# A graph attention layer over sorted edges: the dense part for the first 128 groups is taken out, and feature tiles come free by whole batches

## The chip, the cores and the metric

The kernel runs on one core of a Trainium2 chip. Its time is the device time of one execution in microseconds; the time before is the median of three runs, 6012.39 us (6009.27 to 6016.66). The profile is of one execution, with a line for each instruction: PE is the matrix engine (PEld its weight loads), DVE the vector engine, ACT the scalar engine, POOL the engine that issues the indirect DMAs (gathers), SP an engine that here only issues DMAs.

## The reference

There are 12500 nodes with 64 features, 400000 edges with 64 features each, and the edges are sorted by their destination. The density of destinations falls along the nodes: the first groups of 512 edges lie on a few nodes, the last on some 30.

```python
h_src = nfeats[src]
h_dst = nfeats[dst]
z_att = concatenate([h_src, h_dst, efeats])
e = leaky_relu(z_att @ W_attn + b_attn, 0.01)
m = concatenate([h_src, efeats]) @ W_ne
alpha = exp(e - segment_max(e, dst)[dst]) / segment_sum(exp(...), dst)[dst]
z = segment_sum(alpha * m, dst)
out = layernorm(nfeats + relu(concatenate([nfeats, z]) @ W_out))
```

## The kernel before

The edges are cut into 782 groups of 512 (128 partitions by T = 4; the last group has 128 edges). `sorted_path` (line 48) does the whole work where the destinations are sorted and no group spans more than S = 48 nodes; it leaves a flag, and a second function, `general_path`, runs after it only if the flag is set.

*Setup.* The node table is read, the parts of the score that belong to a node (as source, as destination) are computed, and a table of 65 columns (features and source score) is written to DRAM. A second table in DRAM, `shifted`, holds for each node the destination scores of the 48 nodes from it on; seven gathers (line 525) take from it the window of each group's first node, `wins`.

*Sparse groups.* Groups 127 to 781 (655 of them) go through the loop at line 756 in batches: 16, then 31 of 20 (`BS`), 11 and 8. A batch is worked in parts of `SG` = 4 groups. For each part:

- `gather` (line 199) loads the edges' features `ze` by SP and issues 16 indirect DMAs on POOL, 4 per group, which fetch the table rows of the sources into `zx` (line 214). `ze` and `zx` come from the pool `feats` with `ZB` = 8 buffers each. In the built program each gather also waits for the gather eight before it.
- `scores` (line 220) multiplies `ze` by the edge weights and sums (232, 234), adds the source score (239), marks each edge's destination in a one-hot tile `hot` (241), multiplies it with the window `win` (246) that ACT has copied, and sums (249).

When all parts of a batch have scores, `softmax` (line 294) works on the whole batch: scans along the edges give the maximum and the sum of each destination, and carry over from batch to batch; the weights `alpha` are left in PSUM. Then `aggregate` (line 401) runs part by part: `w` = `hot` times `alpha` on DVE (404, two buffers), 32 products on PE with `ze` and `zx` as weights (412) into `pg` (four PSUM buffers, which other work uses too), and for each group one addition of 48 columns into the accumulator `acc` on DVE (422).

`prepare` (line 739) makes a batch's index lists, two batches ahead: a load, a conversion on ACT, a subtraction on DVE, eight transposes on PE.

*Dense groups.* The first 128 groups never gather: `dense_part` (line 586) is a generator that takes the sources' scores and features from the node table by one-hot products on PE (lines 633, 675, 697), with its own softmax and its own accumulator `acc_d`, merged into `acc` at its end. The loop over the sparse batches takes a step of it after each part's scores, at times two, and one after each part's sums.

*Finishing.* `finish` (line 543) takes four blocks of 128 nodes (25 such blocks of work): transposes of x, products with the output weights, normalisation, and the store. It is due when no later edge can touch its nodes; `due` is computed from the expected distribution of the destinations, and a limit on the actual one is checked into the flag.

The order of the instructions on each engine is laid out by a scheduler when the program is built; each engine then works through its own queue in order.

Of the kernel before, what the change touches and what calls it, by code (L numbers as in the profile page):

```python
# [15 lines left out]
P = 128  # L16
T = 4
# [14 lines left out]
ZB = 8  # L32
HB = 7

DENSE = ((32, 2, (32,)), (32, 2, (13, 10, 9)), (32, 3, (7, 7, 6, 6, 6)), (32, 3, (5, 5, 5, 5, 4, 4, 4)))
KD = 128
ND = 8
NT = 3
NA = 30
NDW = 392  # L40
# [7 lines left out]
def sorted_path(ctx, tc, x, dst, idx, edge, w_ne, w_attn, b_attn, w_out, out, flag):  # L48

# [15 lines left out]
    assert REST == P and NG % BG and sum(G for G, _, _ in DENSE) == KD <= P  # L69
# [18 lines left out]
    slots0 = const.tile([P, P], F32, name="slots0")  # L88
    nc.gpsimd.iota(slots0, pattern=[[1, P]], base=0, channel_multiplier=0,
                   allow_small_or_imprecise_dtypes=True)  # L90
    lane = const.tile([P, 1], F32, name="lane")
    nc.gpsimd.iota(lane, pattern=[[0, 1]], base=0, channel_multiplier=1,
                   allow_small_or_imprecise_dtypes=True)
    ident16 = const.tile([BG, BG], BF16, name="ident16")
    nc.vector.tensor_copy(ident16, ident[0:BG, 0:BG])
    ss = const.tile([P, NB], F32, name="ss")
    ofs = const.tile([1, KD * T], I32, name="ofs")
    at0 = const.tile([1, KD], I32, name="at0")
    acc_d = const.tile([P, NDW], F32, name="acc_d")

# [8 lines left out]
    d0i = const.tile([1, NG], I32, name="d0i")  # L109
    worst = const.tile([P, 2], F32, name="worst")  # L110
    odd = const.tile([1, 4], F32, name="odd")
# [9 lines left out]
    fixed2 = psum.tile([P, 512], F32, name="fixed2", bufs=1)  # L121
# [6 lines left out]
    casts = []  # L128

    def indices(g0, G, dense=False):  # L130

# [11 lines left out]
        lows = None  # L143
        if dense:
            low = dn.tile([P, T, P], F32, name="lot", bufs=2).bitcast(I32)
            nc.vector.tensor_scalar(low[0:G].rearrange("g t (q c) -> g t q c", c=T),
                                    raw[0:G].rearrange("g (t q c) -> g t q c", t=T, c=2 * T)[:, :, :, 0:T],
                                    P - 1, None, op0=OP.bitwise_and)
            lows = chunks.tile([BG, T, P], BF16, name="lows", bufs=1)
            nc.scalar.activation(lows[0:G], low[0:G], AF.Copy)  # L150
        pp = psum.tile([P, 3 * T, BG], F32, name="pp", bufs=1)
        if dense:

            nat = dn.tile([P, NA, NB], F32, name="sums").rearrange("p d h -> p (d h)")[:, 0:2 * T * P]
            nat = nat.rearrange("p (k t e) -> p k t e", k=2, t=T)
            for k in range(2):
                nc.scalar.activation(
                    nat[0:G, k].rearrange("g t (q c) -> g t q c", c=T),
                    raw[0:G].rearrange("g (t q c) -> g t q c", t=T, c=2 * T)[:, :, :, k * T:(k + 1) * T], AF.Copy)
            d4 = tiny.tile([BG, T], F32, name="d4")  # L160
            nc.vector.tensor_copy(d4[0:G], nat[0:G, 1, :, 0])
            for t in range(T):
                nc.tensor.transpose(pp[:, t, 0:G], nat[0:G, 0, t], ident[0:G, 0:G])
            for k, d0 in ((T, [d4[0:G, 0:1]] * T), (2 * T, [d4[0:G, t:t + 1] for t in range(T)])):
                for t in range(T):
                    rel = nat[0:G, 0, t]
                    nc.vector.tensor_scalar(rel, nat[0:G, 1, t], d0[t], None, op0=OP.subtract)
                    nc.tensor.transpose(pp[:, k + t, 0:G], rel, ident[0:G, 0:G])
            srcs = chunks.tile([P, T, BG], I32, name="srcs_d", bufs=1)
            nc.vector.tensor_copy(srcs[:, :, 0:G], pp[:, 0:T, 0:G])  # L170
            return srcs, pp, lows
        nat = raw.bitcast(F32)
        nc.scalar.activation(nat[0:G], raw[0:G], AF.Copy)
        d0 = tiny.tile([BG, 1], F32, name="d0")
        nc.scalar.activation(d0[0:G], nat[0:G, T:T + 1], AF.Copy)
        to = nat[0:G].rearrange("g (p c) -> g c p", c=2 * T)[:, T:2 * T, :]
        nc.vector.tensor_scalar(to, to, d0[0:G], None, op0=OP.subtract)
# [9 lines left out]
    def slots_of(g0, G, pp, wide=S, name="drel", bufs=3, first=T):  # L187

        drel = chunks.tile([P, T, BG], F32, name=name, bufs=bufs)
        nc.scalar.activation(drel[:, :, 0:G], pp[:, first:first + T, 0:G], AF.Copy)  # L190
        if g0 + G == NG:
            nc.vector.memset(drel[RP:2 * RP, :, G - 1:G], -1.0)
            nc.vector.memset(drel[2 * RP:P, :, G - 1:G], -1.0)
        far = tiny.tile([P, 1], F32, name="far")
        nc.vector.tensor_reduce(far, drel[:, :, 0:G], axis=AX.XY, op=OP.max)
        nc.vector.scalar_tensor_tensor(worst[:, 0:1], far, 1.0 - wide, worst[:, 0:1], op0=OP.add, op1=OP.max)
        return drel

    def gather(g0, n, srcs, b0, plain):
# [11 lines left out]
        for g in range(n):  # L211
            for t in range(T):
                at = srcs[:, t, g0 + g - b0:g0 + g - b0 + 1]
                nc.gpsimd.indirect_dma_start(  # L214
                    out=zx[:, g, t, 0:D] if plain else zx[:, g, t, :], out_offset=None,
                    in_=x[:, :] if plain else table[:, :],
                    in_offset=bass.IndirectOffsetOnAxis(ap=at, axis=0))
        return ze, zx
# [54 lines left out]
    def neighbours(g0, G, name="d3", bufs=2):  # L273

        d3 = rows.tile([P, P + 2], I32, name=name, bufs=bufs)
# [18 lines left out]
    def softmax(G, y, d3, carry, first, alpha=alpha, tag="", tiles=False):  # L294
# [24 lines left out]

        e = rows.tile([P, P], F32, name="e")  # L320
        if tiles:
            pe = psum.tile([P, SG, P], F32, name="pg", bufs=4)[:, 0, :]
            nc.tensor.transpose(pe, y.rearrange("p t g -> p (t g)"), ident)
            nc.scalar.activation(e, pe, AF.Copy)
        else:
            er = rows.tile([P, T, P // T], F32, name="er")
            nc.vector.transpose(er.rearrange("r t q -> r (t q)"), y.rearrange("p t g -> p (t g)"))
            nc.scalar.activation(e.rearrange("r (q t) -> r q t", t=T), er.rearrange("r t q -> r q t"), AF.Copy)
# [3 lines left out]
        top = tiny.tile([1, P + 1], F32, name="top" + tag)  # L332
# [9 lines left out]
        def total(s, name):  # L342
# [4 lines left out]
            rt = tiny.tile([1, P + 1], F32, name=f"rt_{name}", bufs=1)  # L347
# [9 lines left out]
        dl = rows.tile([P, P], F32, name="b1")  # L357
# [5 lines left out]
        den = tiny.tile([1, P + 1], F32, name="den" + tag)  # L363
# [13 lines left out]
        al = rows.tile([P, T, P // T], F32, name="er")  # L377
        if tiles:
            al = al.rearrange("r t q -> r (t q)")
            nc.vector.tensor_tensor(al, ex, sm, op=OP.mult)  # L380
            pe = psum.tile([P, SG, P], F32, name="pg", bufs=4)[:, 0, :]
# [869 lines left out]
```

## Time and profile before

| what | value |
|---|---|
| median of three runs | 6012.39 us |
| profiled execution | 6009.27 us |
| its span | 6007.6 us |
| POOL: busy, share | 2492.2 us, 41% |
| DVE: busy, share | 2749.5 us, 46% |
| PE: busy, share | 2414.2 us, 40% |
| ACT: busy, share | 684.8 us, 11% |
| gathers from the table (line 214) | 2556, mean 946 ns |
| POOL idle before them | 3319.9 us |
| last dense instruction on `hot_c` | starts at 5348.6 us |
| first and last gather from the table | 105.6 and 5837.7 us |

Busy time is the time in which an engine has an instruction under way; idle time before a group of instructions is put down to what ended it ("issue" is a wait for nothing that the profile shows, "remote" one whose origin it does not know). The slices are fortieths of the span, some 150 us, and a digit is the busy share in tenths. A row of the time line has the start, the duration, the engine, the line of the kernel and the operation, and in brackets the idle time before it with what ended it. A row of the stretches has busy time and count of PE, PEld, DVE, ACT and POOL in this order, then the clock granted to PE, the share of the DMA engines and GB/s.

### The profile page before, as it was taken

To read this page: it belongs to the slowest core of one execution; us is meant where nothing else is said; L and a number is where in the kernel's file an instruction comes from. 1 tells how busy PE (TensorE), PEld (TensorE's weight loads), DVE (VectorE), ACT (ScalarE), POOL (GpSimd) and SP (SyncE) were. 2 spreads that over 40 slices of the span, in tenths; PEclk is the share of its full clock that TensorE was granted. 3 is DMA by queue.
4 is the path that set the end of the run, shared out by engine and by line. 5 is a ranking of instruction groups with operands and counts; after the bars stand their busy time and mean duration, and the time that the engine had idled before them with its cause. 6 is when DMAs were issued, how large, how long until landed. Compare 5 with 4: busy or idle time off the path is not lost.

```text
span 6007.6 us, 54654 instructions
## 1 busy us (share of the span) xinstructions
PE 2414.2 (40%) x17650; PEld 1801.5 (30%) x17650; DVE 2749.5 (46%) x8457; ACT 684.8 (11%) x1554; POOL 2492.2 (41%) x2635
## 2 busy tenths in 40 slices
PE   0133334443332444442333545643324555453335
PEld 0122222333222333332222333432223343342224
DVE  4345564434556433424456424455543445333445
ACT  0000012110001202100002101210001112110001
POOL 7544434543443444244443343334445333443430
PEclk9755555555555555555555555555555555555555
DMA  6112111112121221221111222221112232222110
GB/s 123 38 40 48 43 34 41 46 42 53 44 47 35 48 57 39 49 56 47 45 44 35 53 62 57 58 60 43 47 42 50 54 71 60 57 68 49 45 35 21
DMA packets 610908, 298.24 MB, mean 50 GB/s; under 512 B 459707, under 2 KB 567911, under 8 KB 610613
## 3 DMA queue, kind: packets, MB, share of 16 engines
q1 hardware_dynamic: 499860, 200.50, 13.3%
q0 software_dynamic: 84064, 87.50, 7.6%
q10 hardware_dynamic: 26688, 6.67, 0.6%
q8 instruction: 142, 2.33, 0.2%
q14 instruction: 154, 1.25, 0.1%
HBM read 287.76 MB, written 9.07 MB: 49 GB/s over the span
## 4 chain that ended last, share of the span: by engine, by line
DVE 23%; issue 22%; PE 20%; another core or an unknown queue 18%; POOL 8%; DMA 5%; ACT 3%; DVEq 1%; SPq 1%; ACTq 0%; POOLq 0%
POOL zx L214 8%; PE pg L412 7%; PE pg L675 5%; DMA ze_d<-in_x_dram 3%; PE pg L697 3%; DVE lot L668 1%; PE pg L678 1%; DVE prod L232 1%; DVE prod L246 1%; ACT hot_c L672 1%; DVE hot L241 1%; ACT hot_c L673 1%; DVE row L260 1%; DVE turn L270 1%
## 5 line engine op out<-in xcount | busy, mean ns | idle before, releaser
L214 POOL DMA_INDIRECT zx<-table,srcs x2556 | 2418.1, 946 | 3319.9 <-PE pg L412 2310.4
L412 PE MATMUL pg<-w,ze 128*64 128x48 f32 x5240 | 708.8, 295 | 956.4 <-issue 583.1
L412 PE MATMUL pg<-w,zx 128*64 128x48 f32 x5240 | 720.1, 296 | 512.9 <-issue 489.2
L422 DVE TENSOR_TENSOR acc<-acc,pg 128x48 f32 x655 | 130.2, 199 | 1724.0 <-remote 980.2
L412 PEld LDWEIGHTS pg<-w,ze 128*64 128x64 f32 x5240 | 604.6, 209 | 1038.1 <-issue 757.8
L412 PEld LDWEIGHTS pg<-w,zx 128*64 128x64 f32 x5240 | 608.0, 207 | 549.2 <-issue 516.8
L675 PE MATMUL pg<-hot_c,lot 128*128 128x196 f32 (+1 forms) x1024 | 569.1, 668 | 441.7 <-ACT hot_c L673 316.3
L633 PE MATMUL pg<-ss,lot 128*128 128x98 f32 x1024 | 259.5, 434 | 750.4 <-DVE lot L630 686.4
L697 PE MATMUL pg<-sums,ze_d 128*64 128x30 f32 x3136 | 388.3, 291 | 357.1 <-DMA ze_d<-in_x_dram 257.3
L697 PEld LDWEIGHTS pg<-sums,ze_d 128*64 128x64 f32 x3136 | 355.4, 220 | 414.5 <-DMA ze_d<-in_x_dram 282.3
L633 PEld LDWEIGHTS pg<-ss,lot 128*128 128x128 f32 x1024 | 227.3, 326 | 826.1 <-DVE lot L630 756.0
L675 PEld LDWEIGHTS pg<-hot_c,lot 128*128 128x128 f32 x1024 | 251.3, 302 | 660.0 <-ACT hot_c L673 530.7
L672 ACT ACTIVATE hot_c<-fixed,code 128x196 f32<-128x196 f32 (+1 forms) x512 | 238.3, 465 | 1748.0 <-DVE lot L668 1055.4
L681 DVE TENSOR_TENSOR sums<-sums,pg 128x196 f32 (+1 forms) x512 | 208.7, 408 | 286.8 <-PE pg L675 123.4
L228 ACT ACTIVATE win<-wrow 128x192 f32<-128x192 f32 x164 | 54.3, 331 | 2334.3 <-DVE lot L630 1187.5
L404 DVE TENSOR_TENSOR w<-hot,fixed 128x768 f32<-128x768 bf16 x164 | 153.9, 946 | 334.4 <-remote 218.5
L668 DVE TENSOR_SCALAR lot<-fixed,lo,al_d 128x128 f32<-128x128 f32 x512 | 204.5, 399 | 196.0 <-ACT hot_c L672 160.6
L673 ACT ACTIVATE hot_c<-hot_c,one_col 128x196 f32<-128x196 f32 (+1 forms) x512 | 255.4, 499 | 16.0
L234 DVE TENSOR_REDUCE y<-prod 128x16 f32<-128x1024 f32 x164 | 198.4, 1210 | 2.3 <-DVE turn L312 1.2
L232 DVE TENSOR_TENSOR prod<-ze,fixed 128x1024 f32<-128x1024 f32 x164 | 198.6, 1211 | 0.0
L246 DVE TENSOR_TENSOR prod<-hot,win 128x768 f32<-128x768 bf16 x164 | 155.1, 946 | 52.0 <-ACT win L228 49.7
L249 DVE TENSOR_REDUCE sdst<-prod 128x16 f32<-128x768 f32 x164 | 154.9, 945 | 5.1 <-remote 2.4
(227 smaller groups left out, 2699.5 us busy)
## 6 DMA issues: line engine op xcount, KB each, us to landing
ze<-in_edge_dram SPq DMA_DIRECT2D x162, 512.0 KB
ze_d<-in_x_dram SPq DMA_DIRECT2D x384, 128.0 KB
zx<-table,srcs POOLq DMA_INDIRECT x2556
ze_d<-in_edge_dram SPq DMA_DIRECT2D x256, 128.0 KB
wrow<-wins SPq DMA_DIRECT2D x157, 96.0 KB
table<-xt ACTq DMA_DIRECT2D x14, 227.5 KB
xb<-in_x_dram ACTq DMA_DIRECT2D x24, 128.0 KB
out_dram<-sq SPq DMA_DIRECT2D x24, 128.0 KB
```

The costliest lines, as they stand in the source:

```text
L214: nc.gpsimd.indirect_dma_start(out=zx[:, g, t, 0:D] if plain else zx[:, g, t, :], out_offset=None, in_=x[:, :] if plain else table[:, :], ...
L232: nc.vector.tensor_tensor(prod[:, 0:n], ze[:, 0:n], w_edge.unsqueeze(1).to_broadcast([P, n, T, D]), op=OP.mult)
L234: nc.vector.tensor_reduce(yb, prod[:, 0:n], axis=AX.X, op=OP.add)
L246: nc.vector.tensor_tensor(at[:, 0:n], hot[:, 0:n], win[:, 0:n].unsqueeze(2).to_broadcast([P, n, T, S]), op=OP.mult)
L412: nc.tensor.matmul(pg[at:at + D, g, :], z[:, g, t, 0:D], w[:, g, t, :], start=(t == 0), stop=(t == T - 1))
L633: nc.tensor.matmul(ps[:, t, :], lot[:, t, :], ss, start=True, stop=True)
L668: nc.vector.tensor_scalar(lo_w[:, t, :], fixed2[:, 0:P], lo[:, t, g:g + 1], al[:, t, g:g + 1], op0=OP.is_equal, op1=OP.mult)
L672: nc.scalar.activation(hot_c[:, 0:wide * NB], fixed2[:, 0:wide * NB], AF.Abs, bias=code[:, t, g:g + 1])
L673: nc.scalar.activation(hot_c[:, 0:wide * NB], hot_c[:, 0:wide * NB], AF.Relu, bias=one_col, scale=-1.0)
L675: nc.tensor.matmul(pa[:, 0:wide * NB], lo_w[:, t, :], hot_c[:, 0:wide * NB], start=True, stop=True)
L681: nc.vector.tensor_tensor(part, part, pa[:, 0:wide * NB].rearrange("l (d h) -> l d h", h=NB), op=OP.add)
L697: nc.tensor.matmul(pf[D:P, 0:NA], xb[:, j, :], sums[:, :, c0 + j], start=(c0 + j == 0), stop=(c0 + j == NB - 1))
```

## The change

- `dense_part`, its constants, tiles, checks and its merge are gone, with the parameters that `indices`, `slots_of`, `neighbours` and `softmax` had for it. All 782 groups go through the sparse loop, in batches of 4, 38 of 20, 10 and 8.
- `feats` has ten buffers (`ZB`). Each gather after the first ten tiles has a dependency on the last sums product of the batch that had the tile ten before: the tiles of a batch come free together. `hot` has eight buffers (seven before), `w` four (two before).
- The scores of a batch's last part are placed on DVE behind the last addition of the batch before (`tc.issue_after(added)`); those of the other parts are left to the scheduler.
- The index lists are loaded and converted two batches ahead at the start of a batch (`listed`), transposed before the batch's last part is summed; destinations are made relative to the group's first by a table `d0b`, which the setup fills by three products, and no longer before the transposes.
- `finish` is cut in two: the load and transposes (`finish1`) stand ahead of a batch's sums, the rest (`finish2`) ahead of the last part's, at most two blocks in a batch, with two buffers for `xb` and `xtt`.

```diff
-ZB = 8
-HB = 7
+ZB = 10
+HB = 8
...
+                if len(owner) >= ZB:
+                    tc.add_manual_dep(got.ins, summed[owner[-ZB]],
+                                      mybir.DependencyInfo(mybir.DependencyClass.Sync, mybir.DependencyReason.DATA),
+                                      reason="the tiles of a batch come free together")
+        owner.append(starts.index(b0))
...
-        w = work.tile([P, SG, T, S], F32, name="w", bufs=2)
+        w = work.tile([P, SG, T, S], F32, name="w", bufs=4)
...
-    left = NG - (KD - 1)
-    for short in (2 * SG, 11):
+    left = NG
+    for short in (2 * SG, 10, 20):
...
-        ready = {k: prepare(k) for k in range(2)}
+        ready = {0: prepare(0), 1: prepare(1, listed(starts[1], sizes[1]))}
         for k, G in enumerate(sizes):
             b0 = starts[k]
             srcs, drel = ready.pop(k)
+            more = k + 2 < len(sizes)
+            nat = listed(starts[k + 2], sizes[k + 2]) if more else None
...
-                hot = scores(g0, n, ze, zx, drel, b0, y, k == 0)
+                with tc.issue_after(added) if added and g0 + SG >= b0 + G else nullcontext():
+                    hot = scores(g0, n, ze, zx, drel, b0, y, k == 0)
                 parts.append((g0, n, ze, zx, hot))
-                if k and running:
-                    steps += 1
-                    running = step(1 + (steps % 4 == 0))
...
-            if k + 2 < len(sizes):
-                ready[k + 2] = prepare(k + 2)
             fac, carry = softmax(G, y, d3, carry, k == 0)
-            for i, (g0, n, ze, zx, hot) in enumerate(parts):
-                aggregate(g0, n, ze, zx, hot, b0, fac if g0 == b0 else None)
-                if k and running:
-                    running = step(1)
...
+            turns = [(c0, *finish1(c0)) for c0 in done[:2]]
+            for g0, n, ze, zx, hot in parts:
+                if g0 == parts[-1][0]:
+                    if more:
+                        ready[k + 2] = prepare(k + 2, nat)
+                    for turn_ in turns:
+                        finish2(*turn_)
+                summed[k], added = aggregate(g0, n, ze, zx, hot, b0, fac if g0 == b0 else None)
+            done = done[2:] + due[k]
```

## The prediction

> **What bounds the kernel now.** I read the busy table and the 40 slices first, then the group of the gathers and what ended their idle time, then POOL and DVE in order of time where no dense work is left, and last the setup and the tail.
>
> ```profile
> PE 2414.2 (40%) x17650; PEld 1801.5 (30%) x17650; DVE 2749.5 (46%) x8457; ACT 684.8 (11%) x1554; POOL 2492.2 (41%) x2635
> POOL 7544434543443444244443343334445333443430
> ...
> L214 POOL DMA_INDIRECT zx<-table,srcs x2556 | 2418.1, 946 | 3319.9 <-PE pg L412 2310.4
> ```
>
> No engine is busy for half of the span. The largest idle time is that of POOL before a gather, and 2310.4 us of it ended with a sums product (line 412). The gathers' own view splits it:
>
> ```profile
> L214 POOL DMA_INDIRECT zx<-table,srcs x2556: 942/947/1231, 105.6 to 5837.7; - x197
> ...
>   PE pg L412: 2310.4, 79
>   issue: 729.7, 2353
>   remote: 189.6, 59
>   PE pg L627: 54.9, 2
> ```
>
> A gather lasts 0.946 us, and 2353 of them came 0.31 us after the one before: alone, POOL makes one every 1.25 us. Beyond that pitch it stood 2310.4 + 189.6 + 54.9 less 140 x 0.31, or 2512 us. The whole adds up: first table gather at 105.6, 2556 x 1.25 = 3195, 2512 of waits, and 170 from the last gather to the end: 5983 of 6007.6.
>
> Dense work ends at 5350, so the last batches show the sparse loop alone:
>
> ```profile
> 5474.73 0.95 POOL L214 DMA_INDIRECT zx<-table,srcs  x1 [65.73 <-PE pg L412]
> 5521.08 0.95 POOL L214 DMA_INDIRECT zx<-table,srcs  x1 [6.63 <-PE pg L412]
> ...
> 5567.69 0.95 POOL L214 DMA_INDIRECT zx<-table,srcs  x1 [6.84 <-PE pg L412]
> 5637.66 0.95 POOL L214 DMA_INDIRECT zx<-table,srcs  x1 [50.25 <-PE pg L412]
> ...
> 5798.97 0.94 POOL L214 DMA_INDIRECT zx<-table,srcs  x1 [53.24 <-PE pg L412]
> ```
>
> A batch of 20 groups takes 162.9 us (5474.73 to 5637.66) though its 80 gathers need 100. The same period stands where dense work runs beside it (357.67 to 520.45: 162.8). So the dense part is not what sets it; the tiles are. A batch needs five tiles, there are eight, and a tile is gathered anew only when its part's products are done; with two w buffers those products wait in DVE's queue among the next batch's scores, which wait for the gathers. POOL so waits once for the softmax (about 50 us) and again tile by tile.
>
> ```profile
> 5474.73:5637.66 162.93, 59.10 (x434) 45.74 (x430) 62.09 (x198) 12.40 (x28) 75.67 (x80) 0.51 0.19 44
> ```
>
> In that stretch DVE (third count) is busy for 62.1 of 162.9 us, POOL (fifth) for 75.7.
>
> **The change, part by part.**
>
> *Dense part out.* Lines 586 to 727 go, with all their DVE, PE, ACT and SP work: on DVE the ten largest groups (L681 208.7, L668 204.5, L630 95.4, L642 71.8, L639 71.1, L643 70.7, L635 52.9, L636 52.9, L653 40.1, L660 22.7) are 891 us. I credit nothing for it in the sum: DVE does not set the end.
>
> *Its 128 groups become sparse.* Gathers rise from 655 x 4 to 782 x 4 = 3128, of which the first batch's 16 come from x in the setup and 3112 from the table. 3112 x 1.25 = 3890 us against 3195, which is 695 us more for POOL.
>
> *Tiles by the batch.* Ten tiles hold two batches. A gather of batch k+2 waits for the last sums product of batch k (call its time M), and stands on POOL behind all gathers of k+1. If G is when the gathers of k end, those of k+1 end at G + 100, so POOL waits only if M is later than G + 100. M, by rows: landing of the last gather, at most 10 us (each gather waits for the one eight before, 8 x 1.25, and the rows show no such wait beyond the pitch), I take 3; the last part's scores 6.3 (5899.58 to 5905.85); softmax 21.8 (5865.90 to 5887.65 below); five w of 0.95, 4.7; products of the last part, 3. M = G + 39, so 61 us are to spare. The 2512 us of waits go. Who is late next: DVE, in its turn, waits for gathers, which costs nothing.
>
> ```profile
> 5865.90 0.31 DVE L327 STREAM_TRANSPOSE er<-y 128x128 f32<-128x128 f32 x1
> ...
> 5887.65 0.95 DVE L404 TENSOR_TENSOR w<-hot,fixed 128x768 f32<-128x768 bf16 x1
> ...
> 5899.58 1.21 DVE L232 TENSOR_TENSOR prod<-ze,fixed 128x1024 f32<-128x1024 f32 x1
> ...
> 5905.85 0.31 DVE L327 STREAM_TRANSPOSE er<-y 128x128 f32<-128x128 f32 x1
> ```
>
> *What stands before M.* In the built program's DVE queue a batch's softmax is followed by four w (four buffers now), one accumulate, the fifth w, three more accumulates, and only then by the first wait for the next batch's gathers. Behind a waiting gather POOL has nothing but later gathers. The other accumulates mix with the scores of the next batch's first four parts; the fifth part's scores stand behind the last of them (`issue_after(added)`). With four PSUM buffers the fifth part's products need the first part's accumulates, which stand before that wait. In the 22 batches that carry a finishing block they need the second part's too, behind a gather landed by G + 23 and some 8 us of DVE: still before M. So the new waits (POOL on PE, last scores on the last accumulate) cost nothing while M keeps its 61 us; without that cover each microsecond counts 39 times.
>
> *DVE.* A part costs 1.21 + 1.21 + 0.95 + 0.95 + 0.95 (scores), 0.95 (w), 4 x 0.20 (accumulates) and three small ones of 0.18: 7.5 us, a batch 37.7 + 21.8 + about 1 of index work = 60 of 100 us. It would set the pace only at 1.6 times these durations.
>
> *Loads.* Edge loads (SP) come free with each part's products, a batch or more before they are needed; ACT's and SP's moved loads (list of indices, xb) stand ahead of work that needs them a batch later. Traffic is 5.3 MB per 100 us, 53 GB/s; slices of before reached 71. Between 30 and 60 us POOL issued 24 gathers at a DMA share of 1.13, so a burst of loads does not stretch the pitch.
>
> *Setup.* 16 plain gathers instead of 64 end before the window table is ready. That transfer left at 61.5 and the DMA share fell from 1.14 to 0.13 by 80; seven gathers on it follow, 8.8 us. First table gather: between 88 and the 105.6 of before; I take 90, since both queues otherwise keep their order.
>
> *Tail.* Before: the last gather at 5837.7, then seven finishing blocks in a row of 9.6 us each, the end at 6007.6. After: the last two batches have 10 and 8 groups, two blocks are left over, two run in the batch ahead. Batch 39 (10 groups) must get through softmax, products and two blocks before the last part's scores: these reach DVE some 16 us after the last gather. Then 3.5 to the softmax, 21, from w to the flag 8.3 (5932.09 to 5940.4), two blocks 9.5, last operation to the end 6.4: 65. Bounds: 50 if DVE is free when the last gather lands, 85 with two more blocks' time.
>
> **A rule weighed.** The gathers of the table have a median of 947 ns and a maximum of 1231 with DVE busy for 46% of the span; the only slower ones are three of the first from x, in the setup:
>
> ```profile
> 11.65 1.89 POOL L214 DMA_INDIRECT zx<-in_x_dram,srcs  x1 [0.30 <-issue]
> ```
>
> The Trainium skill (SBUF — State Buffer, section "SBUF: two separate sides", the box on the "DVE blocks DMA" trap) says that a DMA issued from GpSimd can't write its descriptors while VectorE holds a shared port pair in a two-port mode; it gives about 3100 ns for one under such a copy. By it, gathers that always met one would take 3112 x 3.4, over 10 ms. The trace shows at most 1.231 us among 2556, so I keep 1.25.
>
> **Sum.** 90 + 3890 + 65 = 4045 us of span. The profiled run was 6009.27 for a span of 6007.6 (1.7 around it), and the median of three is 0.05% above it: 4045 + 2 + 2 = 4049, say 4050 us.
>
> **Rivals.**
>
> A, the forecast: POOL streams. 4050, own range 4005 to 4110 (first gather 88 to 106, tail 50 to 85, pitch 1.245 to 1.256).
>
> B, it streams with hitches, as tiles today start 3.2 us late ("remote" 189.6 / 59) even when free. Once a batch, 39 x 3 = 117: 4170; before each of 195 tiles, 585: 4635. For it: those rows. Against: every wait of a tile's first gather but the first is on work a batch old.
>
> C, the batch keeps its period because a wait that I place before M stands behind gathers. 39 x 162.9 + 155 = 6510, slower. It decides from a period of 150 us ((6012 - 155) / 39), 50 us of POOL waiting per batch, that is, M at G + 150. For it: two dense-free batches at 162.9 and 161.3. Against: the queue order above.
>
> D, gathers stretch beside denser scores. At the 2.19 us pitch of the setup's three slow ones (11.65, 13.85, 16.05): 3112 x 2.19 + 155 = 6970. It decides at a pitch of 1.88. Against: 1.231 at most in 5.7 ms.
>
> E, the change doesn't do what it says: the second path runs as well, if a limit it computes (48 slots a group, early blocks) is exceeded. It has no row in the trace; it can't be a gain, and its gathers of every edge alone would add as much again, 4050 + 3910 = 7960.
>
> **How the numbers follow.** A 0.85, B 0.09, C 0.03, D 0.02, E 0.01. Predicted: A's 4050. The range takes A and the mild form of B: 4005 to 4180. Faster (by over 0.2%, what this kernel's spread of 6009 to 6017 can tell from none): A + B, 0.94; C to E slower, 0.055; same 0.005.
>
> **What the profile would show.** Right: POOL near 73% busy with one digit from end to end, 3112 gathers whose idle time is nearly all "issue" at 0.30, a batch every 100 us, DVE near 60% with its waits ended by gathers; no waits of the gathers on line 358. Wrong: gathers that wait for sums products once a batch (C), a mean well over 0.95 us (D), lines above 590 (E). The first table gather and the last one's distance from the end check the setup and the tail.

## The result and the profile after

The changed kernel took **5285.99 us** (median of four, 5279.3 to 5287.15) against 6014.52 for the kernel before (6009.27 to 6016.66): ratio **0.879**, 95% interval 0.877 to 0.880. The direction was forecast, the size was not: 4050 was forecast, within 4005 to 4180.

Ahead of everything else stands one fact that the experiments brought out: the time of both kernels changes with the chip that a set of runs came to. Each set of runs below has runs of the kernel before on its own chip:

| sets of runs | kernel before, us | changed kernel, us |
|---|---|---|
| the result | 6014.52 | 5285.99 |
| six sets, on five chips | 3926 to 3931 (single runs 3918 to 3939) | 4236.44 (timed in one of the sets) |
| one set (`e10_traffic`) | 6008.92 | not run |
| one set (`t_pause`) | 6042.33 | not run |

I call the first and the last two *holding* chips and the other five *quiet* chips; why is seen below. The runs of one set agree with each other, and one chip came up in two of the sets, quiet both times; which chip gave the result is not known, so whether it is the chip or something that passes on it no run shows. The clock granted to PE does not tell the two apart: 0.573 in the result's profile, and 0.573 in that of `e6_srcs4` on a quiet chip. On the quiet chip where both were timed, the change makes the kernel **slower**: 4236.44 against 3926.44, ratio 1.079, interval 1.077 to 1.081. So the verdict of the result belongs to the kind of chip that gave it. Times are compared below only between runs whose kernel before took the same time.

The page of the changed kernel, from the result: busy times, POOL's forty slices, the groups of the gathers and of one small copy of the softmax (busy, mean ns of one, then idle time before them and what ended most of it).

```profile
PE 657.6 (12%) x13346; PEld 612.9 (12%) x13346; DVE 2211.2 (42%) x6612; ACT 245.8 (5%) x527; POOL 2978.4 (56%) x3142
...
POOL 4745555556555555555555555555555555555550
...
L167 POOL DMA_INDIRECT zx<-table,srcs x3112 | 2948.1, 947 | 2109.0 <-PE pg L358 1140.7
...
L218 DVE COPY row<-tr 1x32 f32<-1x32 f32 x656 | 137.5, 210 | 847.2 <-issue 671.5
```

POOL was to be 73% busy with one digit from end to end; it is 56%. The gathers have the forecast 947 ns, but 1140.7 us were spent waiting for a sums product (line 358), 37 times. In order of time, each batch shows it once; a gather follows the one before without a gap until the tiles run out:

```profile
2037.85 0.94 POOL L167 DMA_INDIRECT zx<-table,srcs  x1 [29.26 <-PE pg L358]
...
2136.72 0.94 POOL L167 DMA_INDIRECT zx<-table,srcs  x1 [0.30 <-issue]
2168.72 0.94 POOL L167 DMA_INDIRECT zx<-table,srcs  x1 [31.06 <-PE pg L358]
```

A batch takes 130.9 us (2037.85 to 2168.72) where 100 were forecast. What is late is the softmax. DVE's rows beside those gathers (start, duration, and in brackets the idle time before and its end):

```profile
2064.61 0.21 DVE L215 STREAM_TRANSPOSE tr<-s 128x32 f32<-128x32 f32 x1 [1.91 <-remote]
2065.32 0.18 DVE L218 COPY row<-tr 1x32 f32<-1x32 f32 x1 [0.49 <-DVE tr L215]
2067.39 0.19 DVE L218 COPY row<-tr 1x32 f32<-1x32 f32 x1 [1.89 <-issue]
2068.79 0.18 DVE L218 COPY row<-tr 1x32 f32<-1x32 f32 x1 [1.21 <-issue]
2070.20 0.19 DVE L218 COPY row<-tr 1x32 f32<-1x32 f32 x1 [1.23 <-issue]
2072.29 0.47 DVE L290 TENSOR_TENSOR_SCAN top<-rw,top,row 1x128 f32<-1x128 f32 x1 [1.90 <-issue]
```

A copy lasts 0.18 us, but the next starts 1.40 us after it, with nothing that it waits for. Starts lie 0.70 or a multiple of it apart (1.40, 1.41, 2.07, 2.09). So the softmax, from the transposition `er` to the first `w`, takes 93 us (2060.42 to 2153.43) where I had put 21.8. Large operations show nothing of it: the products and reductions of the scores follow each other without a gap in the same profile. The small operations that stand among them don't either, 13 us into the same gathers:

```profile
2050.47 0.20 DVE L368 TENSOR_TENSOR acc<-acc,pg 128x48 f32 x1
2050.58 0.19 DVE L197 TENSOR_TENSOR y<-y,zx 128x16 f32<-128x16 f32 x1
2050.69 0.95 DVE L199 TENSOR_TENSOR hot<-fixed,drel 128x768 bf16<-128x768 f32 x1
```

In the 22.6 us from the first gather to `er` DVE starts 47 instructions; the steps come only behind them. And three of the 41 softmaxes in this profile have no gather beside them, the second and the last two: they take 19.6, 19.3 and 18.7 us.

The same program on a quiet chip, same lines, beside gathers as well:

```profile
1999.85 0.99 DVE L218 COPY row<-tr 1x32 f32<-1x32 f32 x4
2000.88 0.47 DVE L325 TENSOR_TENSOR_SCAN den<-rw,den,row 1x128 f32<-1x128 f32 x1
2001.39 0.92 DVE L228 COPY turn<-den 1x32 f32<-1x32 f32 x4
```

Four copies in 0.99 us. Over the whole run, 783 of DVE's instructions start 1.38 to 1.42 us after the one ahead of them on the holding chip; on the quiet one it is one instruction.

**The kernel before has the same trouble in another place.** Waits of its sums products and of its gathers, first on the result's chip, then on a quiet one (total us, times, longest):

```profile
POOL zx L214 <- PE pg L412: 2310.4, 79, 94.5
PEld pg L412 <- issue: 1274.5, 1176, 28.2
...
PE pg L412 <- issue: 1072.3, 1135, 14.5
```

```profile
POOL zx L214 <- PE pg L412: 497.2, 29, 45.0
...
PEld pg L412 <- issue: 162.5, 46, 29.6
...
PE pg L412 <- issue: 51.9, 11, 14.5
```

On the holding chip the products on PE come in the same steps, as its rows beside gathers show:

```profile
5101.20 0.24 PE L412 MATMUL pg<-w,zx 128*64 128x48 f32 x1 [0.95 <-issue]
5101.91 0.33 PE L412 MATMUL pg<-w,zx 128*64 128x48 f32 x1 [0.47 <-issue]
5102.59 0.24 PE L412 MATMUL pg<-w,ze 128*64 128x48 f32 x1 [0.36 <-issue]
5103.30 0.34 PE L412 MATMUL pg<-w,ze 128*64 128x48 f32 x1 [0.47 <-issue]
```

That is what the change moved. Medians over the batches from the tenth on (of the kernel before to the 29th, as long as dense work runs beside them), read from the rows; the first line counts to the start of the last product:

| | before, holding | before, quiet | after, holding | after, quiet |
|---|---|---|---|---|
| first `w` to the last sums product, us | 97.9 | 32.8 | 14.8 | 14.8 |
| gathers that start in that time | 63 | 22.5 | 0 | 12 |
| from one softmax to the next, us | 181.6 | 116.2 | 131.4 | 100.1 |

Before, tiles came free one by one, so gathers ran beside the products and held them, and the gathers then waited for the products. After, POOL stands still while the products run on the holding chip, and it is the softmax that runs beside the gathers. Holding costs the kernel before 65 us a batch (181.6 against 116.2) and the changed one 31 (131.4 against 100.1), because the gathers go on beside the held softmax until the tiles run out. Over the whole runs that is 6014.52 - 3926.44 = 2088 us against 5285.99 - 4236.44 = 1050: the change saves 1038 us of holding and loses the 310 that it loses on a quiet chip. That is the 12%. On a quiet chip nothing is held; the change only trades the dense part for 556 more gathers, 695 us of POOL, and gets back less.

### The profile page after: what moved, and what is told of

It reads as the page before. It is cut to its first block, busy times and chain, and to the rows that moved or that the text cites. A ratio compares the mean times of both kernels' runs of the same rounds, so it can differ in the third digit from the quotient of the medians.

```text
span 5277.6 us, 40966 instructions
## 1 busy us (share of the span) xinstructions
PE 657.6 (12%) x13346; PEld 612.9 (12%) x13346; DVE 2211.2 (42%) x6612; ACT 245.8 (5%) x527; POOL 2978.4 (56%) x3142
## 4 chain that ended last, share of the span: by engine, by line
issue 58%; DVE 26%; PE 7%; another core or an unknown queue 4%; DMA 2%; POOL 1%; DVEq 1%; SPq 1%; ACT 0%; ACTq 0%
PE pg L358 5%; DVE prod L190 2%; DVE hot L199 2%; DVE acc L368 2%; DVE row L218 2%; DVE turn L228 1%; DVE sdst L207 1%; DVE y L192 1%; DVE tr L215 1%; DVE prod L204 1%; POOL zx L167 1%; PE pg L505 1%; PE pg L504 1%; DMA zx<-table,srcs 1%
## 5 line engine op out<-in xcount | busy, mean ns | idle before, releaser
L167 POOL DMA_INDIRECT zx<-table,srcs x3112 | 2948.1, 947 | 2109.0 <-PE pg L358 1140.7
L358 PE MATMUL pg<-w,ze 128*64 128x48 f32 x6256 | 476.5, 249 | 3669.8 <-DVE w L350 2103.7
L358 PEld LDWEIGHTS pg<-w,ze 128*64 128x64 f32 x6256 | 468.6, 167 | 3674.9 <-DVE w L350 2007.4
L218 DVE COPY row<-tr 1x32 f32<-1x32 f32 x656 | 137.5, 210 | 847.2 <-issue 671.5
L358 PE MATMUL pg<-w,zx 128*64 128x48 f32 x6256 | 477.5, 249 | 25.7 <-issue 25.7
L358 PEld LDWEIGHTS pg<-w,zx 128*64 128x64 f32 x6256 | 468.3, 167 | 28.8 <-issue 28.8
L192 DVE TENSOR_REDUCE y<-prod 128x16 f32<-128x1024 f32 x196 | 237.4, 1211 | 3.2 <-remote 3.2
L199 DVE TENSOR_TENSOR hot<-fixed,drel 128x768 bf16<-128x768 f32 x196 | 185.8, 948 | 0.0
L131 PE MATMUL pp<-ident,nat 20*128 20x20 f32 (+3 forms) x328 | 42.6, 269 | 716.3 <-DVE sdst L207 241.0
L134 DVE CAST srcs<-pp 128x80 int32<-128x80 f32 (+3 forms) x41 | 9.8, 238 | 249.4 <-DMA zx<-table,srcs 246.5
L505 PE MATMUL pg<-both,acc 128*128 128x64 f32 x196 | 64.4, 430 | 97.7 <-DVE acc L368 82.1
```

Source lines behind the costliest of these rows:

```text
L167: got = nc.gpsimd.indirect_dma_start(out=zx[:, g, t, 0:D] if plain else zx[:, g, t, :], out_offset=None, in_=x[:, :] if plain else table[: ...
L192: nc.vector.tensor_reduce(yb, prod[:, 0:n], axis=AX.X, op=OP.add)
L199: nc.vector.tensor_tensor(hot[:, 0:n], slots.unsqueeze(1).unsqueeze(1).to_broadcast([P, n, T, S]), drel[:, :, b:b + n].rearrange("p t g -> ...
L218: nc.vector.tensor_copy(row.rearrange("o (g h) -> o h g", h=HQ)[:, h, :], tr[h * BG:h * BG + 1, :])
L358: last = nc.tensor.matmul(pg[at:at + D, g, :], z[:, g, t, 0:D], w[:, g, t, :], start=(t == 0), stop=(t == T - 1))
L505: nc.tensor.matmul(po[:, j, :], acc[:, (c0 + j) * P:(c0 + j + 1) * P], both, start=False, stop=True)
```

## Experiments

All runs but `e10_traffic` and `t_pause` were made on quiet chips. Times are medians with their lowest and highest where a kernel was timed more than once.

**No gather beside a softmax.**

```diff
+                if starts.index(b0) >= 1:
+                    tc.add_manual_dep(got.ins, ended[starts.index(b0) - 1], ...)
...
-        nc.vector.transpose(alpha0..., al...)
+        ended.append(nc.vector.transpose(alpha0..., al...).ins.name)
```

> The gathers of a batch wait for the last operation of the softmax of the batch ahead, so no gather runs beside a softmax. Theory 'held copies': beside the gathers VectorE's small SBUF-to-SBUF copies of the softmax are each held for about 1.2 us, and that is why the batch ends at 131 us and not at 100. Then the softmax takes about 22 to 25 us here in place of 93, and a batch is 100 of gathers + 3 of landing + 6 of the last part's scores + 22 to 25 of softmax = 131 to 134 us: the time stays within 3% of the changed kernel's 5286 us (5280 to 5430), though the gathers and the softmax no longer overlap at all. Rival 'slow in itself' (the softmax takes 93 us wherever it stands, for its waits or its code): a batch is 100 + 9 + 93 = 202 us, in all about 8060 us.

Measured on a quiet chip: 4922.56 us (4920.74 to 4923.98), softmax 19.5 to 21.3 us, 121.5 us a batch. My estimate of 131 to 134 took the last part's scores as 6 us after the landing; in truth `er` follows the last gather by 3.5 us, because all that does not need the rows is done before they land. So the softmax is not slow by its own code. What it says of holding had to wait for the other kind of chip (`t_pause`).

**Maximum in place of the plain copies.**

```diff
-            nc.vector.tensor_copy(row...[:, h, :], tr[h * BG:h * BG + 1, :])
+            nc.vector.tensor_tensor(row...[:, h, :], tr[...], tr[...], op=OP.max)
```

The copies in `to_col`, those to `rw` and those of `fac1` likewise.

> The 36 copies a batch of one to three rows of 32 within the softmax are written as the maximum of the source with itself: same engine, same sizes, same count and same order of work, two inputs in place of one. Theory 'held copies', in the form that it is the plain copy that is held: only the ten transposes and two or three copies are left to be held, some 12 x 1.2 us over the 22 us that the softmax takes alone, so 30 to 45 us; the last sums product then comes before the last gather and a batch takes 100 us: about 4080 us, 4050 to 4150. Rival 'any small VectorE operation beside the gathers is held, whatever its form': softmax 93 us, 131 us a batch, 5286 us as before. Rival 'two inputs from SBUF are held as well, and longer': over 5300 us.

4259.92 us (4258.3 to 4261.5): neither number. No small operation was held, and the softmax took about 21 us from the ninth batch on, but 92 to 94 us in batches 2 to 8, by a single wait amid it (below). I nearly took this as a proof that copies are held and maxima are not. The run of the unchanged kernel on such a chip (`r_after`) showed that copies are not held there either; the experiment told nothing of them.

**No gathers in the loop.**

```diff
+        if not plain:
+            for g in range(n):
+                nc.sync.dma_start(out=zx[:, g], in_=table[q0 + g * P:q0 + g * P + GE, :]...)
-        for g in range(n):
+        for g in range(n if plain else 0):
```

> From the second batch on the 80 gathers of a batch are replaced by 20 plain loads of as many table rows on SP's queue (so the rows that are read are the wrong ones); GpSimd does nothing in the loop. Theory 'held copies': the softmax takes 22 to 25 us, and VectorE, busy 55 us a batch, sets the pace: 58 to 70 us a batch, in all 2400 to 3000 us. Rival 'slow in itself': the softmax stays near 93 us, at least 110 us a batch with the parts beside it, 4400 us or more.

2404.8 us, softmax 19.5 to 20.4, DVE busy 90%. A batch takes 54 to 60 us, at the lower end of what was expected: that is DVE's own pace.

**No softmax.**

```diff
-            fac, carry = softmax(G, y, d3, carry, k == 0)
+            nc.scalar.activation(alpha, y, AF.Copy)
+            fac = None
```

> The softmax is left out: one copy of the scores on ScalarE stands in its place (and the loads of destinations for it are gone). What is left of the prediction's sum is then alone: 90 + 3112 x 1.25 + 65 = 4045 us, if the gathers can run on end at 1.25 us; 4000 to 4100 us. Rival 'the gathers themselves can't run on end': the held copies came every 1.40 us and were held up to 12 us after a batch's last gather, as if a gather cost 1.40 us behind its row; then 3112 x 1.40 + 155 = 4510 us. Rival 'the tiles come free late whatever the softmax does': 5286 us as before.

4018.06 us, and POOL's digits are those that the forecast wanted:

```profile
POOL 2777777777777777777777777777777777777774
...
L167 POOL DMA_INDIRECT zx<-table,srcs x3112 | 2937.4, 944 | 948.2 <-issue 922.0
```

3119 gathers run on end at 1.249 us, so the pitch and the tiles of the sum were sound, and on this chip the gathers do not cost 1.40 us.

**Both kernels as they are, on a quiet chip; and the maximum with four index buffers.**

> The changed kernel as it is, timed and profiled beside the experiments, because the kernel before took 3927 us beside the first experiments and 6014 us beside the result. If the chip that runs the experiments does not hold the softmax's copies, the changed kernel is faster here as well: softmax 20 to 30 us, 4020 to 4270 us, and the experiment with the maximum in place of the copies has then shown nothing of the copies. If it holds them as in the result, softmax 83 to 97 us and 5286 us again within 1%.

> The kernel before as it is, for its profile on the chip of the experiments: 3927 us. Where the 2087 us less come from is to be read in it: if it is the same cause as in the changed kernel, then the copies within the softmax and within the dense part that were held in the profile of the result (softmax 21 to 52 us a batch there) stand here without a gap, and POOL's waits for a tile, 2310 us there, are nearly gone. Rival: the gathers' pitch or VectorE's durations differ (1.25 us and 0.95 to 1.21 us there).

`r_after`: 4236.44 us (4235.91 to 4236.78). `r_before`: 3938.54 us; pitch (1.25 us) and DVE's durations are unchanged, and POOL's waits for products fell from 2310.4 to 497.2, shown above. So of the 2071 us between the two profiled runs, 1813 are this wait. The expectation named the wrong work, though: the softmaxes of the kernel before take 21 to 52 us on both chips (medians 33.4 us over the batches of the table above). On the holding chip hardly a gather runs beside them; what was held there is the sums products.

`r_after` still waits seven times for products, 193.1 us, all in the first batches, and there the softmax takes 91 to 99 us. One row stands amid it:

```profile
550.67 0.24 DVE L134 CAST srcs<-pp 128x80 int32<-128x80 f32 x1 [71.82 <-DMA zx<-table,srcs]
```

The conversion of the indices two batches ahead (line 134) writes one of three buffers, which gathers of the batch still under way read; the scheduler had put it in the middle of the softmax, and DVE's queue is in order.

> The experiment with the maximum in place of the copies, with four buffers in place of three for the indices (bufs of srcs). In it no copy was held, but the first seven batches lost 28 us each where the conversion of the indices two batches ahead, put amid the softmax, waited 73 us for gathers that still read the same buffer. With a fourth buffer that wait goes: 4260 - 8 x 28 = 4036 us, 4010 to 4060. Rival: another wait of the same kind takes its place and the time stays above 4150 us.

4045.33 us (4044.67 to 4046.45): the wait is gone.

**Four index buffers alone.**

```diff
-        srcs = chunks.tile([P, T, BG], I32, name="srcs", bufs=3)
+        srcs = chunks.tile([P, T, BG], I32, name="srcs", bufs=4)
```

> The changed kernel with four buffers for the indices in place of three (bufs of srcs), and nothing else. If the kernel before takes 3927 us beside it, as beside the last two sets of runs: the conversion of the indices no longer waits amid the softmax of the first batches, the maximum in place of the copies had no part in it, and the time is that of the experiment with both, 4045 us (4030 to 4060). If the maximum did have a part, 4150 us or more. If the kernel before takes 6014 us beside it, as beside the result: the held copies remain, 83 us of softmax a batch, and the time falls by at most 6 waits of 28 us: 5100 to 5286 us.

4044.18 us (4042.65 to 4046.26), ratio to the kernel before 1.029. The maximum had no part in it.

```profile
POOL 3777777777777777777777777777777777777773
...
L167 POOL DMA_INDIRECT zx<-table,srcs x3112 | 2945.9, 947 | 948.5 <-issue 912.5
```

This is the forecast's kernel: POOL streams, 4044 against 4050.

**A longer softmax with nothing held.** The last reciprocal of the softmax, on top of four index buffers, repeated in place (an odd number of times, so the result stays):

```diff
-        nc.vector.reciprocal(sm, sm)
+        for _ in range(67):
+            nc.vector.reciprocal(sm, sm)
```

> The changed kernel with four index buffers (4044 us) and with 66 more reciprocals on the chain of the softmax, at the row's 0.95 us 63 us: the softmax takes 21 + 64 = 85 us, as it does in the profile of the result, but nothing is held. Theory 'VectorE's queue is the pacer': a batch on VectorE is the softmax and then, in the same queue, the sums of this batch mixed with the scores of the next, 36 us from the first w to the next er in the profile of the result (2024.85 to 2060.42); a batch then takes 85 + 36 to 45 = 121 to 130 us, and the time is 4044 + 40 x 21 to 30 = 4880 to 5250 us: the length of the softmax alone gives nearly all of the result's 5286. Rival 'other engines' work is held as well and counts' (sums, landings): clearly less than 4880 us. Rival by the prediction's own sum (the last sums product comes at G + 39 with a softmax of 21.8, so at G + 103 here, 3 us a batch too late): 4160 us.

> The same with 32 more reciprocals, so a softmax of 21 + 31 = 52 us. Theory 'VectorE's queue is the pacer': 52 + 36 to 45 = 88 to 97 us, under the 100 us of the gathers, so nothing is lost: 4044 us (4030 to 4080). Rival 'the sums product was already just in time': each us of softmax costs one, 4044 + 40 x 31 = 5284 us.

`e7_pad_long`: softmax 86 us, 5124.33 us, 124 us a batch on the mean. DVE is busy 93% and POOL waits in the same place as in the result:

```profile
POOL zx L167 <- issue: 887.8, 2913, 0.3
...
POOL zx L167 <- PE pg L359: 860.9, 36, 30.2
```

`e8_pad_short` (33 times): softmax 52 us, 4135.67 us. POOL never waits for a product; the 91 us over 4044 lie behind the last gather (148.4 us to the end in place of 57.7), where the last three softmaxes are no longer hidden, 31 us each. So a softmax of 52 us is free as long as gathers follow, and one of 86 costs 24 us a batch: length alone costs 5124 - 4044 = 1080 us, most of the 1242 by which the result lies above 4044.

**The kernel before with four index buffers** (the edit of `e6_srcs4` in the kernel before).

> The kernel before, with four buffers in place of three for the indices. Its profile beside these experiments has VectorE waiting 245 us, 14 times, for gathers that still read the buffer that the conversion of the indices is to write, and POOL waiting 497 us for sums products. If the one wait feeds the other as in the changed kernel, 3927 - 245 to 3927 - 100: 3680 to 3830 us, faster than both kernels. Rival: those waits lie beside the dense part's work and another takes their place: 3927 us within 1%.

**3756.78 us** (3753.25 to 3759.82), ratio 0.956 (0.954 to 0.958): on a quiet chip faster than both kernels. POOL's waits for products fell from 497.2 to 343.2 us.

**More traffic.** Four transfers of 512 KB a part, from DRAM to DRAM, on ACT's queue, in the kernel with four index buffers:

```diff
+        for j in range(4):
+            junk = spare.tile([P, 1024], F32, name="junk", bufs=8)
+            nc.scalar.dma_start(out=junk, in_=edge[j * 2048:(j + 1) * 2048, :]...)
```

> Still open: what held the instructions on the chip of the result. This is the kernel with four index buffers (4044 us, softmax 21 us) with four more transfers of 512 KB each a part, DRAM to DRAM on ScalarE's queue: 10 MB more read and as much written a batch, some 200 GB/s over 100 us where the kernel alone moves 60. Theory 'other traffic holds them' (on the result's chip something else kept the DMA engines or the memory busy): VectorE's small instructions then come with gaps of 0.70 and 1.40 us here too, the softmax grows beyond 30 us, and the time with it. Rival 'it is not the traffic': the softmax stays at 20 to 23 us, without such gaps; loads and gathers may land later and move the time, but not the softmax.

This set came to a holding chip: the kernel before took 6008.92 us, this one 5357.48. The transfers ran ahead of the loop and were over at about 2950 us, so the profile has both halves. In the first eight batches, where traffic is densest and the gathers come in short bursts, the softmax takes anything from 40 to 128 us; from the ninth on it takes 84 to 94 us while the traffic lasts and 79 to 93 after it, and a batch 131 us. So the steps need no such traffic, and here it makes them no worse; whether traffic could make a quiet chip hold was not tried. On this chip a fourth index buffer does not take the steps away.

**On a holding chip: is it the gathers?** Four kernels, three of them for the second time, came to a quiet chip:

> Again the kernel in which the gathers of a batch wait for the softmax ahead, for a chip on which the kernel before takes 6014 us and the changed kernel 5286. Theory 'held beside the gathers': on that chip VectorE issues small instructions only every 0.70 or 1.40 us while GpSimd makes gathers, and at its own pace else. Without gathers beside it the softmax takes 20 to 23 us there too, and the whole 4900 to 5000 us as on the other chip (4923): 6% faster than the changed kernel, by waiting. Rival 'that chip holds instructions whatever GpSimd does': softmax above 60 us, over 6500 us. Where the kernel before takes 3927 us: 4923 us once more, and nothing is learnt.

> Again the maximum in place of the plain copies, with four index buffers, for the same chip. Theory 'issue is held, whatever the instruction': the 36 small two-input operations are held as the copies were, softmax 80 to 95 us, about 5260 us. Rival 'plain copies alone are held' (by a lock on a port that GpSimd shares): softmax 21 to 40 us, 4040 to 4150 us. Where the kernel before takes 3927 us: 4045 us once more.

> Again the kernel before with four index buffers, for the same chip. There its time goes into sums products and small operations that are held beside the gathers and not into the buffer of the indices, so it should gain little: 5900 to 6014 us. Where the kernel before takes 3927 us: 3757 us once more.

> The changed kernel with four index buffers, and with the row and column turns of the softmax on TensorE: a product with a reordered identity gives the row at once, four small products the column, in place of a transpose and four copies on VectorE each. Some 45 of the softmax's 85 VectorE instructions go, and 9 copies of a column or a row come. Theory 'issue is held, per instruction': on the chip with 6014 us some 40 VectorE instructions and 8 hops to TensorE are left, 45 to 65 us of softmax; with the 36 us for sums and scores that is 81 to 101 us a batch, so 4050 to 4150 us there, 21% faster than the changed kernel. Rival 'it is the time and not the count': the softmax stays above 75 us, over 5000 us. On the chip with 3927 us: 4045 us (the gathers set the pace), with a softmax of 20 to 28 us.

4920.94, 4043.58, 3763.92 and 4037.74 us: the first three as before; in the fourth the softmax is down to 15 us, which the gathers hide anyway. It replaces the turns by products on PE:

```diff
-        tr = rows.tile([P, BG], F32, name="tr")
-        nc.vector.transpose(tr, block)
-        for h in range(HQ): nc.vector.tensor_copy(...)
+        nc.tensor.matmul(aux[0:1, 0:P], block[:, 0:1], order..., start=True, stop=True)
```

Then the kernel without gathers beside the softmax once more, alone:

> Once more the kernel in which no gather runs beside a softmax, for a chip on which the kernel before takes 6014 us. Theory 'held beside the gathers': softmax 20 to 23 us there too, 4900 to 5000 us in all, 6% faster than the changed kernel there. Rival 'that chip holds instructions whatever GpSimd does': softmax above 60 us, over 6500 us. Where the kernel before takes 3927 us: 4921 us, and nothing is learnt.

This was a holding chip: 6042.33 for the kernel before, 6419.13 for this one. The softmax takes **19.5 us** there:

```profile
1984.08 0.30 DVE L284 STREAM_TRANSPOSE er<-y 128x128 f32<-128x128 f32 x1
...
2003.59 3.55 DVE L355 TENSOR_TENSOR w<-hot,fixed 128x768 f32<-128x768 bf16 x4
```

So it is not the chip alone: without gathers beside it the softmax is not held. But the whole became slower, which neither theory said. The work that now runs beside the gathers is the sums products. From the first `w` to the last product it is 120.3 us with 79 gathers beside (27.2 on a quiet chip, `e1_pause`), in the same steps:

```profile
2012.07 0.32 PE L363 MATMUL pg<-w,zx 128*64 128x48 f32 x1
2012.76 0.24 PE L363 MATMUL pg<-w,ze 128*64 128x48 f32 x1 [0.35 <-issue]
2013.46 0.34 PE L363 MATMUL pg<-w,zx 128*64 128x48 f32 x1 [0.47 <-issue]
2014.16 0.24 PE L363 MATMUL pg<-w,zx 128*64 128x48 f32 x1 [0.36 <-issue]
2014.85 0.24 PE L363 MATMUL pg<-w,ze 128*64 128x48 f32 x1 [0.46 <-issue]
...
2115.87 0.34 PE L363 MATMUL pg<-w,zx 128*64 128x48 f32 x1
2115.99 0.31 PE L363 MATMUL pg<-w,ze 128*64 128x48 f32 x1
2116.00 0.31 PE L363 MATMUL pg<-w,zx 128*64 128x48 f32 x1
```

At 2115.9 the products fall back to two in 0.11 us. Holding follows the gathers and hits the small work beside them, on DVE and on PE. It does not begin with the first gather: 59 products start from 2004.64 to 2007.76, one every 0.05 us, beside the first four gathers and ahead of the first step.

> Once more the kernel with the softmax's turns on TensorE, for a chip on which the kernel before takes 6014 to 6042 us. Theory 'small instructions of any engine are held beside the gathers': the softmax still runs beside the gathers, with 40 VectorE instructions in place of 85 and some 50 small ones of TensorE: 45 to 70 us, so 81 to 115 us a batch and 4100 to 4700 us, 11 to 22% faster than the changed kernel there. Rival 'it is the time and not the count': the softmax stays above 75 us, over 5000 us. Where the kernel before takes 3927 us: 4038 us once more, and nothing is learnt.

It came to a quiet chip, 4037.29 us. Whether fewer small instructions would win on a holding chip stays open, as does `e9_before_srcs4` there.

## Why the prediction was wrong

- **The failed term is the softmax of 21.8 us in M** (and in DVE's 60 us). I read it from 5865.90 to 5887.65, behind the last gather of the run (5837.7), and put it beside gathers, where it takes 82 to 97 us on that chip (batches 3 to 38). DVE's queue around it was forecast nearly right. On the means of batches 10 to 38, `e7_pad_long` has 86.0 of softmax and 38.1 of everything else, 124.1, and 37.7 was forecast for the rest; the result has 87.0 and 44.1, 131.0. The 6 us more are small operations at the end of a batch's scores, which are held as well (in the batch after the one shown, 2191.41 to 2200.97).
- *The cover was too large as well.* M = G + 39 left 61 us, so a softmax of up to 83 us would have been free. But the softmax and the next batch's scores stand in one queue, and the prediction's own figures for DVE leave it only 100 - 37.7 - 1 = 61 us, 39 more than 21.8. `e8_pad_short` (52, free) and `e7_pad_long` (86, 24 us a batch, where M's spare would have left 3) lie on both sides of that bound and fit it. I had both figures and used the looser one.
- *What that costs.* 37 waits of 1140.7 us less 37 x 0.31 of pitch, 1129; one wait of 31 for a finishing product (line 495); the tail 135.5 in place of 65, 71; the pitch, 1.2525 in place of 1.25, 8. Less 5 for the first table gather (85.3 in place of 90) that is 1234, and 5286 - 4050 is 1236.
- *Right:* the pitch (947 ns and 0.31), 3112 gathers, the first table gather within 5 us (85.3 for 90, just under the stated 88), the last part's scores behind the additions at no cost, the tail where nothing is held (57.7 in `e6_srcs4`, within 50 to 85), and that a second path does not run.
- *Missed on every chip:* the index buffer. The prediction let POOL and DVE wait only for the tiles; line 134 writes a buffer that gathers two batches back read. On a quiet chip it costs 4236 - 4044 = 192 us; in the result only six such waits remain (246.5 us), under the held softmax.
- *Why before waits.* I wrote that the tiles set its period. They do, but I put the wait down to products that stand among the next batch's scores; on that chip it is mostly the products themselves, stretched from 33 to 98 us a batch. The line `PE pg L412 <- issue`, 1135 waits, stood in the list of waits. A wait for nothing, a thousand times over, on an engine that is 40% busy, was worth a look at its rows. The first batch's softmax in that trace, at 183.8 with the last gathers just ahead of it, already took 33 us (21 in `r_before`).
- *What set the period before.* I also wrote that the dense part does not set it, from one batch of 162.8 us beside dense work. That reading was too narrow: the tenth to the 29th batch have a median of 181.6 and up to 226, against 156 and 161 in two batches behind the dense part. It does not enter the sum.
- *The direction is in part luck.* The wait that the change was to remove, 2310.4 us for sums products, is 497.2 on a quiet chip, and there the change loses. Nothing in the prediction told the two cases apart.
- *Rival C* (a wait ahead of M keeps the batch's period) is nearest to what happened: POOL waits 31 us a batch, under the 50 from which it would have lost. Its mechanism, waits for the next batch's gathers, was not it.
- *The rule weighed.* I took the Trainium skill's page "SBUF — State Buffer" (section "SBUF: two separate sides") in one direction only, VectorE stopping GpSimd's descriptors, and found none: the gathers keep 0.947 us here too, even beside the softmax. The same section also says that whichever of a VectorE instruction in a two-port mode and a GpSimd instruction starts first gets the shared pair, and the other blocks. That would fit held copies on DVE, but not the runs: on a quiet chip the same copies beside the same gathers are not held (four in 0.99 us), and on holding chips PE's products are, of which the section says that PE waits for no one. So this rule is not shown to be the cause.

What makes a chip hold is open. Shown is that on such a chip the small instructions of the softmax, and the sums products, start in steps of 0.70 us when gathers run beside them; that the gathers and the large operations keep their own pace; and that a softmax with no gather beside it is not held.

## What to carry to other kernels

Take a duration from rows that stand beside the work it will stand beside after the change; the same softmax took 19.5 and 93 us on one kind of chip. When a list of waits shows an engine waiting for nothing hundreds of times, look at those rows for a step, and time the kernel on a second chip: here the sign of the change depends on it. And before a wait is put down to data, look for a buffer that work two batches ahead wants to write: one more index buffer was worth 4.4% to the kernel before on a quiet chip.

## What was not expected of the hardware

- Two kinds of chip: the kernel before takes 3918 to 3939 us on five and 6009 to 6042 on the others, with the same durations of the gathers (946 and 948 ns) and of DVE's products for the scores (1.21 us).
- On the holding ones, steps of 0.70 us between small instructions on DVE and PE beside indirect DMAs of GpSimd. They start late: behind 59 products of PE in `t_pause`, and behind 47 instructions of DVE, small ones among them, in the result. Whether the engines draw on something made ready ahead until then no run shows.
- The steps outlast the gathers: 80 gathers from 2003.5 to 2103.1 hold PE until 2115.9 in `t_pause`, and in the result 80 gathers from 2037.85 to 2137.7 hold DVE until 2148.6. Both are about 1.4 us a gather counted from the first, though the gathers themselves keep 1.25 and their last rows land some 2 us after the last issue. What is at work in those last 11 to 13 us no run shows.
